# Second biases of the experts by one transpose and one wide matmul in both mixtures of layer 0, and the shared expert four parts later in the first

## The chip, the cores and the metric

The kernel runs on one core of one Trainium2 chip, all in float32. The core has a matrix engine (TensorE; PE in the profile, with its weight loads as PEld), a vector engine (VectorE, DVE), a scalar engine (ScalarE, ACT), a general engine (GpSimd, POOL) and a queue engine (SyncE, SP). Each works through its own list of instructions in order; they wait for each other by semaphores. TensorE writes only to PSUM, a small memory from which DVE and ACT read; GpSimd does not reach it. The metric is the device time of one execution in microseconds (us); lower is better.

## What is computed

The input x is 4 blocks of 512 tokens with 128 channels. It passes through four layers, each a half-weighted mixture or feed-forward part, an attention, and the mixture again. The change touches the two mixtures of layer 0, which share their weights. For one mixture, cut to what matters:

```python
x = x + 0.5 * ffn(layernorm(x))

def ffn(x):                                   # all tokens, 8 experts, 2 of them for each token
    scores = softmax(x @ gate_w.T)
    _, idx = top_k(scores + gate_b, 2)
    comb = (take(scores, idx) one-hot over the experts)     # [token, expert]
    for each expert e:
        h = swiglu((x @ w1[e] + b1[e]) * (x @ w3[e] + b3[e]))
        routed += comb[:, e, None] * (h @ w2[e] + b2[e])
    shared = swiglu((x @ sw1 + sb1) * (x @ sw3 + sb3)) @ sw2 + sb2
    return routed + shared
```

The sum over the experts of comb[:, e] * b2[e], with the shared expert's sb2 as a ninth row, does not need the experts' hidden values. It is one small product for each block: the combination weights (512 tokens by 9) times the second biases (9 by 128).

## The kernel before

One block of 512 tokens is four groups of 128 tokens (NT = 4, P = 128), with the token on the partition. The weights of layer 0 are loaded once. The kernel is written as Python generators: each `yield` ends a part, and the order in which parts are stepped is the order in which instructions are handed to a scheduler. The scheduler puts them in order on each engine by its own estimates, and may move them; only inside the attentions is TensorE's order kept as written (`manual_schedule`). Tiles come from pools with a fixed number of buffers; a new use of a buffer waits for the readers of the old one.

**`route(b)`** (L467) does the routing of one block: layernorm, transpose (L310) and its copy to SBUF (L477), the gate's logits (L485), softmax on ACT and DVE, the rank of each expert for each token (`ranks`, L333 to L338, on DVE), the taken experts (L496), matmuls that count how many tokens stand ahead for each expert (L503, L505), row numbers (L508 to L513), and then eight scatters of 128 rows each by GpSimd into `sorted_x`, sorted by expert (L551). Four closures hold the work on the combination weights:

- `weigh` (L516) sets the ninth column of `comb` to 0.5 on DVE (L517) and the other eight to half the score where the expert is taken (L518), and keeps each token's two shares (L520 to L523).
- `across` (L529) turns `comb`, one group of 128 tokens at a time, with four matmuls against the identity into one PSUM tile of 9 x 512 (L532), and copies it to SBUF on ACT (L533).
- `biases` (L535) multiplies it by the bias rows, again one matmul per group, into a PSUM tile of 128 x 512 (L538).
- `into` (L541) adds that to x on DVE (L321).

`comb` comes from the pool `tiny` with four buffers. In the first mixture the closures run after the eight scatters; in the second, the routes of blocks 0 to 2 are `slow`: they run beside the attention of a later block, and the closures are spread between the scatters.

**`common(b)`** (L563) is the shared expert for one block: eight matmuls of 512 columns (L571) in four pairs, each pair into one two-bank PSUM tile `big` (three buffers), a scaled copy on ACT (L573), products and clamps on DVE (L576 to L584), a sigmoid on ACT (L581), eight matmuls back (L589), and an addition into x (L591). **`fold`** (L594) rewrites the first weights of the eight experts (sixteen matmuls L600, eight copies L601), so that biases ride along, and then loads a row of biases (L603). **`plan`** (L605) computes which expert tile holds what, sends the table through TensorE (L661) to SP and TensorE (L663), and fills the ends of the experts' rooms with zeros (L616). **`tiles`** (L695) then goes through 39 tiles of 128 sorted rows, two at a time: rows fetched by SP (L705), turned (L716), first weights (L726), activation (ACT L729, L738; DVE L733 to L742), turned again (L751), second weights (L759), stored (L763). `places` (L665) computes, on DVE, from which rows each token gathers its results; `back` (L796) gathers them on GpSimd (L807) and adds them (L802).

In the first mixture, the four routes are stepped together, each block four rounds behind the one before, and the chain of `fold` and the four shared experts joins in from round 5:

```python
rest = chain(fold, *shared)
for k in range(24):
    for b in range(B):
        if k >= 4 * b:
            step(routes[b])
    if k > 4:
        step(rest)
```

Between the mixtures stands the attention of layer 0: a head pair at a time, scores (L1035), exponentials on ACT (L1036), sums of them on DVE (L1044), and values (L1049), with the projections of the next pair (L985, L996).

Of the kernel before, what the change touches and what calls it, by code (L numbers as in the profile page):

```python
# [11 lines left out]
F32 = mybir.dt.float32  # L12
# [5 lines left out]
P = 128  # L18
B, S, D = 4, 512, 128
NT = S // P  # L20
EPS = 1e-5
NE = 8
# [104 lines left out]
def laid_out(i):  # L127
    a = {"x": i["L0_attn_x"].reshape(B * S, D)}

    def both(k):  # L130
        return np.concatenate([i[f"L0_ffn_{k}"], i[f"L0_ffn_s{k}"][None]])

    n = NE + 1

    w13 = [both(k).reshape(n, D, L0_I, 2).transpose(1, 0, 3, 2) for k in ("w1", "w3")]
    a["w13"] = np.stack(w13, axis=2)
    b13 = [i[f"L0_ffn_{k}"].reshape(NE, L0_I, 2).transpose(0, 2, 1) for k in ("b1", "b3")]
    a["b13"] = np.stack(b13, axis=1).reshape(1, NE, 2, 2, L0_I)
    for k in ("b1", "b3"):
        a[k] = both(k).reshape(n, 2, P, 2).transpose(2, 0, 3, 1)  # L140
    a["bs"] = np.stack([a[k][:, NE] for k in ("b1", "b3")], axis=1)
    a["w2"] = both("w2").reshape(n, 2, P, D).transpose(2, 0, 1, 3)
    a["b2"] = both("b2")
    a["gate_w"] = i["L0_ffn_gate_w"].T
    a["gate_b"] = i["L0_ffn_gate_b"][None]

    a["w_down"] = np.concatenate([i["L0_attn_w_down_q"], i["L0_attn_w_down_kv"]]).T
    up = []
    for k in ("q", "k"):
        w = i[f"L0_attn_w_up_{k}"]  # L150
        swapped = w.reshape(-1, 2, w.shape[1])[:, ::-1].reshape(w.shape)
        up.append(np.stack([w.T, swapped.T], axis=1))
    a["w_up_qk"] = np.concatenate(up)
    a["w_up_v"] = i["L0_attn_w_up_v"].T
    a["w_up_v_pairs"] = i["L0_attn_w_up_v"].reshape(L0_H // 2, P, 64).transpose(1, 0, 2)
    a["w_out"] = i["L0_attn_w_out"].T.reshape(L0_H // 2, P, D).transpose(1, 0, 2)
    a["ln_scale"] = i["L0_attn_ln_scale"][:, None]
    a["ln_bias"] = i["L0_attn_ln_bias"][:, None]

    a["l1_wqkv"] = np.concatenate([i[f"L1_attn_W{k}"] for k in "qkv"]).T  # L160
    a["l1_bqkv"] = np.concatenate([i[f"L1_attn_b{k}"] for k in "qkv"])[None]
    a["l1_wo"] = i["L1_attn_Wo"].T
    a["l1_bo"] = i["L1_attn_bo"][None]
    a["l1_beta"] = i["L1_attn_beta"][None]
    a["router_w"] = i["L1_ffn_router_w"].T
    a["lora_down"] = i["L1_ffn_lora_down"].reshape(P, D).T
    a["lora_up"] = i["L1_ffn_lora_up"].transpose(0, 2, 1).reshape(P, D)


    def pad_cols(w):  # L170
        out = np.zeros((D, H, 32), np.float32)
        out[:, :, :DH] = w.reshape(D, H, DH)
        return out.reshape(D, NG * P)

    def pad_rows(w):
        out = np.zeros((NJ, 32, NG, D), np.float32)
        out[:, :DH] = w.reshape(NG, NJ, DH, D).transpose(1, 2, 0, 3)
        return out.reshape(P, NG, D)

    def pad_bias(v, one):  # L180
        out = np.zeros((NJ, 32, NG), np.float32)
        out[:, :DH] = v.reshape(NG, NJ, DH).transpose(1, 2, 0)
        out[:, DH] = one
        return out.reshape(P, NG)

    for n, pre, t in (("l2", "L2_attn_W_", False), ("l3", "L3_attn_W", True)):
        w = {k: i[pre + k].T if t else i[pre + k] for k in "qkvo"}
        v = {k: i[pre.replace("W", "b") + k] for k in "qkvo"}
        a[n + "_wq"], a[n + "_wk"] = pad_cols(w["q"]), pad_cols(w["k"])
        a[n + "_bq"], a[n + "_bk"] = pad_bias(v["q"], 0.0), pad_bias(v["k"], 1.0)  # L190

        for k in "qk":
            a[n + "_w" + k + "s"] = w[k].reshape(D, NG, NJ, DH).transpose(0, 2, 1, 3).reshape(D, P)
            a[n + "_b" + k + "s"] = v[k].reshape(NG, NJ, DH).transpose(1, 0, 2).reshape(P, 1)
        a[n + "_wv"], a[n + "_bv"] = w["v"], v["v"][None]
        a[n + "_wo"], a[n + "_bo"] = pad_rows(w["o"]), v["o"][None]
    a["l2_wg"] = i["L2_ffn_Wg"]
    a["l2_w1"] = i["L2_ffn_W1"].transpose(1, 0, 2)
    a["l2_w2"] = i["L2_ffn_W2"].reshape(NE, HID // P, P, D).transpose(2, 0, 1, 3)
    for k in "rkv":  # L200
        a["l3f_w" + k] = i["L3_ffn_W_" + k].T
    a["l3_mu"] = np.stack([i["L3_ffn_mu_r"], i["L3_ffn_mu_k"]], axis=1)
    a.update({"c_" + k: v for k, v in shape_constants().items()})
    return {k: np.ascontiguousarray(v) for k, v in a.items()}
# [34 lines left out]
def program(ctx: ExitStack, tc: tile.TileContext, a: dict, out: bass.AP, worst):  # L239

    nc = tc.nc
# [3 lines left out]
    tiny = SimpleNamespace(tile=lambda *args, **kw: smalls[-1].tile(*args, **kw))  # L245
# [187 lines left out]
    def by_expert(w, rooms, key):  # L433
# [33 lines left out]
        def route(b, work, rows_pool=None, slow=False):  # L467
# [43 lines left out]
            nc.vector.tensor_tensor(mine, m12[:, b], at.unsqueeze(1).to_broadcast([P, 2, NT, NE]), ALU.mult)  # L511
            nc.vector.tensor_reduce(rows[:, b], mine, AX.X, ALU.add)
            nc.vector.tensor_copy(irows[:, b], rows[:, b])  # L513
            comb = tiny.tile([P, NT, NE + 1], F32, tag="comb", name="comb")

            def weigh():  # L516
                nc.vector.memset(comb[:, :, NE], 0.5)  # L517
# [5 lines left out]
                nc.vector.tensor_scalar(share[:, b], share[:, b], 0.5, None, ALU.mult)  # L523


            combT = work.tile([NE + 1, S], F32, tag="combT", name="combT")
            held = []

            def across():  # L529
                pc = one()  # L530
                for t in range(NT):
                    nc.tensor.matmul(pc[: NE + 1, t * P : (t + 1) * P], lhsT=comb[:, t, :], rhs=ident, start=True, stop=True)  # L532
                nc.scalar.copy(combT, pc[: NE + 1, :])  # L533

            def biases():  # L535
                pb = one()
                for t in range(NT):
                    nc.tensor.matmul(pb[:, t * P : (t + 1) * P], lhsT=combT[:, t * P : (t + 1) * P], rhs=w["b2"], start=True, stop=True)  # L538
                held.append(pb)

            def into():  # L541
# [1371 lines left out]
    with tc.tile_pool(name="w0", bufs=1, reuse_waits="tile") as wp:  # L1913
# [9 lines left out]
        else:  # L1923
# [5 lines left out]

            w0["w_up_qk"] = head.tile([P, L0_H * L0_DH], F32, tag="w_up_qk", name="w_up_qk")  # L1930
            behind.append((w0["w_up_qk"], a["w_up_qk"][:, 0, :]))
            w0.update(loads(wp, ["w13", "bs", "w2", "b2"], later=later))
            later += behind
            dram = ctx.enter_context(tc.tile_pool(name="rooms", bufs=1, space=bass.MemoryType.DRAM))
            rooms = [dram.tile([r, D], F32, tag=t, name=t) for t, r in (("sorted_x", ROOM * NE), ("sorted_y", NTL * P))]
# [1 line left out]
            with tc.tile_pool(name="work", bufs=1, reuse_waits="tile") as work:  # L1937
                w0.update(loads(work, ["c_less"]))
                t, src = later.pop(0)
                for e in ((NE, NE + 1), (0, NE // 2), (NE // 2, NE)):  # L1940
                    nc.sync.dma_start(out=t[:, e[0] : e[1]], in_=src[:, e[0] : e[1]])
                w0.update(loads(work, ["c_place", "c_stride"]))
                pairs = load(work, "w_up_v_pairs", later=later)
                for t, src in later[:3]:
                    nc.sync.dma_start(out=t, in_=src)
                mix = by_expert(w0, rooms, 1)
                routes = [mix.route(b, wp, work if b == B - 1 else None) for b in range(B)]
                shared = [mix.common(b, work) for b in range(B)]
                fold = mix.fold()

                rest = chain(fold, *shared)
                for k in range(24):
                    for b in range(B):
                        if k >= 4 * b:
                            step(routes[b])
                    if k > 4:
                        step(rest)
                finish(chain(*routes))
                iwho, places = mix.plan(work)
                finish(rest)  # L1960

                made = {}
                pair01 = {}, {}

                def projected():
                    raw, qk = pair01
                    for n in range(2):
                        raw[n] = l0_project(n, made[0][0], w0, head)
                        yield
                    qk[0] = l0_turned(w0, *raw[0])  # L1970
                    yield

                first, second = chain(places, mix.back(0, wp), l0_begin(0, w0, head, made, 1), projected()), mix.back(1, wp)
                for _ in mix.tiles(work, iwho, later[3:]):
                    if not mix.ready(0):
                        step(places)
                    elif next(first, first) is first and mix.ready(1):
                        step(second)
                values_to_outputs(w0, pairs)
                finish(chain(first, second))  # L1980

                zeros = work.tile([P, D], F32, tag="zeros", name="zeros")
                nc.gpsimd.memset(zeros, 0.0)
                for px, py in pair_rooms:
                    for e in range(NE):
                        nc.sync.dma_start(out=px[e * P : (e + 1) * P, :], in_=zeros)
                        nc.sync.dma_start(out=py[2 * S + e * P : 2 * S + (e + 1) * P, :], in_=zeros)
# [131 lines left out]
```

## Time and profile before

| | us |
|---|---|
| median of 5 runs | 1463.8 |
| lowest and highest run | 1455.44, 1466.82 |
| the profiled execution | 1462.89 |
| its span, first to last instruction | 1461.0 |
| TensorE busy in the span | 1286.4 (88%) |
| DVE busy | 962.8 (66%) |
| ACT busy | 649.7 (44%) |
| POOL busy | 289.9 (20%) |
| L538, 64 records: busy | 9.2 |
| L532, 64 records: busy | 8.9 |
| L533, 8 copies of 9 x 512: mean of one | 0.574 |
| mean granted clock of TensorE, of full speed | 0.926 |

The profile is of one execution, so all places in time below are its own. Stages, in us from its start: first mixture 0 to about 210 (routing and shared expert up to 91, then expert tiles), attention about 210 to 570, second mixture's last block, shared expert and plan about 570 to 623, then its expert tiles. A line of a timeline gives start, length, engine, source line, operation, output and input tiles, shapes, count, and in brackets how long the engine had been idle and what released it. A float32 matmul leaves two records on PE, a transpose one. In the table of stretches, after the stretch and its length come the busy times of PE, PEld, DVE, ACT and POOL with the number of instructions, then the granted clock (1.00 is full speed), the share of the DMA engines and GB/s.

### The profile page before, as it was taken

The numbers are of one execution on the slowest core, as the hardware profiler recorded it, in microseconds if no ns is written. First come the engines' busy times: TensorE is split into PE (matmuls) and PEld (weight loads), VectorE is DVE, ScalarE is ACT, GpSimd is POOL, SyncE is SP. The second block draws the span as 40 slices with busy tenths as digits, with TensorE's granted clock in tenths as the row PEclk, the third lists the DMA queues.
The fourth block names the chain that finished last, engine by engine and source line by source line (L and its number), as shares of the span: only waits on it lengthen the run. The fifth ranks groups of instructions, "written<-read, shape, count | busy, mean of one in ns | idle before, by whom it ended". The sixth has DMA issues, their size and how long they took to land.

```text
span 1461.0 us, 20212 instructions
## 1 busy us (share of the span) xinstructions
PE 1286.4 (88%) x7078; PEld 680.1 (47%) x7078; DVE 962.8 (66%) x2348; ACT 649.7 (44%) x925; POOL 289.9 (20%) x271
## 2 busy tenths in 40 slices
PE   6999889999999999899876598789887899899995
PEld 3556453344353435455544485453554344443233
DVE  4796678989888885876775546467555744355324
ACT  2445436635455453254543242435343436444561
POOL 3510420323112020202343112220212120210000
PEclk9999989999999998999987697899799989989997
DMA  7123211201111020112114000010001000100000
GB/s 271 41 72 98 65 52 58 80 36 71 51 44 72 31 76 1 40 55 60 30 47 168 1 1 1 30 30 1 7 24 29 1 8 22 30 0 9 8 8 11
DMA packets 59970, 63.52 MB, mean 43 GB/s; under 512 B 11082, under 2 KB 51284, under 8 KB 59220
## 3 DMA queue, kind: packets, MB, share of 16 engines
q1 hardware_dynamic: 54228, 50.60, 10.2%
q0 software_dynamic: 5632, 11.55, 2.6%
q8 instruction: 59, 0.97, 0.3%
q14 instruction: 51, 0.41, 0.1%
HBM read 28.69 MB, written 16.65 MB: 31 GB/s over the span
## 4 chain that ended last, share of the span: by engine, by line
PE 67%; DVE 16%; issue 7%; ACT 4%; POOL 3%; DMA 1%; another core or an unknown queue 0%; POOLq 0%; ACTq 0%; DVEq 0%; SPq 0%
PE big L1035 8%; PE one L1049 7%; PE big L1454 7%; PE big L726 6%; PE one L1467 6%; PE big L571 2%; PE one L1078 2%; ACT pT L1457 2%; PE big L985 2%; PE one L759 2%; PE one L1489 2%; PE one L310 2%; PE big L1813 1%; POOL rs L290 1%; PE one L1827 1%
## 5 line engine op out<-in xcount | busy, mean ns | idle before, releaser
L1457 ACT ACTIVATE pT<-big 128x1024 f32<-128x1024 f32 (+3 forms) x256 | 205.7, 865 | 241.8 <-PE big L1454 215.0
L1454 PE MATMUL big<-qkq,qkk 32*128 32x512 f32 (+3 forms) x1024 | 179.3, 583 | 31.3 <-ACT pT L1457 15.7
L1036 ACT ACTIVATE pT<-big 128x1024 f32<-128x1024 f32 x128 | 125.7, 1034 | 55.1 <-PE big L1035 50.2
L726 PE MATMUL big<-w_w,xsT 128*128 x312 | 148.9, 600 | 0.4 <-issue 0.3
L290 POOL TENSOR_TENSOR rs<-rs,root 128x4 f32<-128x4 f32 x51 | 56.9, 1116 | 424.8 <-DVE rs L289 411.1
L1035 PE MATMUL big<-qk 64*128 64x512 f32 x512 | 129.7, 614 | 6.8 <-DVE U L1071 6.8
L1467 PE MATMUL one<-pT,V 128*32 128x512 f32 (+3 forms) x1024 | 126.7, 581 | 1.3 <-DVE pT L1461 0.9
L1454 PEld LDWEIGHTS big<-qkq,qkk 32*128 32x128 f32 x1024 | 65.5, 195 | 120.3 <-ACT pT L1457 45.1
L807 POOL DMA_INDIRECT yg<-sorted_y,ito x64 | 72.2, 1127 | 228.7 <-DMA sorted_y<-ys 152.3
L1049 PE MATMUL one<-pT,V 128*64 128x512 f32 x512 | 116.9, 598 | 0.0
L551 POOL DMA_INDIRECT sorted_x<-xn,irows x64 | 72.5, 1133 | 70.3 <-DVE share L523 23.9
L1044 DVE TENSOR_TENSOR sums<-sums,pT 128x1024 f32<-128x1024 f32 x64 | 78.1, 1221 | 4.8 <-ACT pT L1036 0.4
L1035 PEld LDWEIGHTS big<-qk 64*128 64x128 f32 x512 | 47.3, 189 | 70.2 <-issue 42.3
L1461 DVE TENSOR_TENSOR pT<-pT,w_c_tri 128x256 f32<-128x256 f32 x128 | 51.8, 421 | 36.6 <-ACT pT L1457 31.6
L726 PEld LDWEIGHTS big<-w_w,xsT 128*128 128x128 f32 x312 | 53.9, 193 | 40.0 <-issue 40.0
L1605 DVE COPY U<-one 128x512 f32<-128x512 f32 x32 | 22.1, 689 | 72.5 <-PE one L1467 67.3
L1049 PEld LDWEIGHTS one<-pT,V 128*64 128x64 f32 x512 | 33.9, 136 | 75.2 <-issue 71.2
L1467 PEld LDWEIGHTS one<-pT,V 128*32 128x32 f32 x1024 | 30.0, 118 | 81.4 <-issue 61.1
L733 DVE TENSOR_TENSOR us<-big,t1s 128x1024 f32<-128x1024 f32 (+1 forms) x40 | 47.8, 1194 | 23.8 <-PE one L716 18.8
L571 PE MATMUL big<-xnT,w_w 128*128 128x512 f32 x128 | 60.6, 608 | 3.0 <-DVE u L576 3.0
L1126 ACT COPY U<-one 128x512 f32<-128x512 f32 x32 | 18.8, 587 | 95.0 <-PE one L1049 85.4
L321 DVE TENSOR_TENSOR x<-x,one 128x512 f32<-128x512 f32 x31 | 21.2, 685 | 55.0 <-PE one L1078 19.0
(344 smaller groups left out, 2333.6 us busy)
## 6 DMA issues: line engine op xcount, KB each, us to landing
other<-qk SPq DMA_DIRECT2D x64, 256.0 KB
xs<-sorted_x SPq DMA_DIRECT2D x78, 64.0 KB
sorted_y<-ys SPq DMA_DIRECT2D x38, 128.0 KB
w_w<-in_w SPq DMA_DIRECT2D x2, 2048.0 KB
w_l_w<-in_l_w SPq DMA_DIRECT2D x2, 2048.0 KB
X<-pair_x SPq DMA_DIRECT2D x3, 512.0 KB
pair_y<-y SPq DMA_DIRECT2D x6, 256.0 KB
w_w<-in_w SPq DMA_DIRECT2D x1, 1152.0 KB
```

The source lines that it names most:

```text
L290: nc.gpsimd.tensor_tensor(rs, rs, root, ALU.pow)
L551: apart(nc.gpsimd.indirect_dma_start(out=sorted_x[:, :], out_offset=bass.IndirectOffsetOnAxis(ap=irows[:, b, j, t : t + 1], axis=0), in_=x ...
L571: nc.tensor.matmul(pa[:, m, :], lhsT=w["w13"][:, NE, m, odd, c * P : (c + 1) * P], rhs=xTs[b], start=True, stop=True)
L726: nc.tensor.matmul(pa[:, k, :], lhsT=st[u]["xT"][:, k * P : (k + 1) * P], rhs=w["w13"][:, bass.ds(st[u]["e"][k], 1), m].rearrange("p o a b ...
L807: nc.gpsimd.indirect_dma_start(out=y, out_offset=None, in_=sorted_y[: done(b) * P, :], in_offset=bass.IndirectOffsetOnAxis(ap=ito[:, b, j, ...
L1035: nc.tensor.matmul(sT[:, u, :], lhsT=k[r, t * P : (t + 1) * P], rhs=q[r, :], start=True, stop=True)
L1036: nc.scalar.activation(pT[:, :, t % 2, :], sT, AF.Exp, scale=scale)
L1044: nc.vector.tensor_tensor(s, s, pT[:, :, m, :], ALU.add)
L1049: nc.tensor.matmul(po[r, :], lhsT=V[:, t, :], rhs=pT[:, u, t % 2, :], start=(t == 0), stop=(t == NT - 1), tile_position=(0, 64 * u))
L1454: nc.tensor.matmul(sT[j // 2][:, j % 2, :n], lhsT=kT[r, t * P : (t + 1) * P], rhs=qT[r, S - n :], start=True, stop=True)
L1457: nc.scalar.activation(pT[j2][:, :, :n], sT[j2][:, :, :n], AF.Exp, scale=scale)
L1467: nc.tensor.matmul(po[32 * j : 32 * j + 32, S - n :], lhsT=V[k % 2][:, t, NJ * g + j, :], rhs=pT[j // 2][:, j % 2, :n], start=(t == 0), st ...
```

## The change

The combination weights of a block are laid out with 32 columns for each group of 128 tokens instead of 9, four groups side by side: 128 x 128, of which the unused columns are zero. `across` then needs one transpose, and the turned tile has partition 32 t + e for group t and expert e. The bias rows are laid out by the host as a matrix of 128 x 512 (`b2_wide`), in which row 32 t + e holds expert e's bias in the 128 columns of group t and zeros elsewhere. `biases` is then one matmul of 512 columns with all 128 rows summed. The zeros of `comb` are set by a memset on GpSimd; `comb` gets two buffers instead of four. The load of `b2` becomes one of `b2_wide`. In the first mixture, `fold` and the shared experts join the routes from round 9 instead of round 5.

```diff
@@ laid_out
     a["b2"] = both("b2")
+
+    wide = np.zeros((NT, 32, NT, D), np.float32)
+    for t in range(NT):
+        wide[t, :n, t] = a["b2"]
+    a["b2_wide"] = wide.reshape(P, NT * D)
@@ route
-            comb = tiny.tile([P, NT, NE + 1], F32, tag="comb", name="comb")
+            comb = tiny.tile([P, NT, 32], F32, tag="comb", name="comb", bufs=2)
+            nc.gpsimd.memset(comb, 0.0)
...
-            combT = work.tile([NE + 1, S], F32, tag="combT", name="combT")
+            combT = work.tile([P, P], F32, tag="combT", name="combT")
             held = []
 
             def across():
                 pc = one()
-                for t in range(NT):
-                    nc.tensor.matmul(pc[: NE + 1, t * P : (t + 1) * P], lhsT=comb[:, t, :], rhs=ident, start=True, stop=True)
-                nc.scalar.copy(combT, pc[: NE + 1, :])
+                nc.tensor.transpose(pc[:, :P], comb.rearrange("p t e -> p (t e)"), ident)
+                nc.scalar.copy(combT, pc[:, :P])
 
             def biases():
                 pb = one()
-                for t in range(NT):
-                    nc.tensor.matmul(pb[:, t * P : (t + 1) * P], lhsT=combT[:, t * P : (t + 1) * P], rhs=w["b2"], start=True, stop=True)
+                nc.tensor.matmul(pb, lhsT=combT, rhs=w["b2_wide"], start=True, stop=True)
                 held.append(pb)
@@ program
-            w0.update(loads(wp, ["w13", "bs", "w2", "b2"], later=later))
+            w0.update(loads(wp, ["w13", "bs", "w2", "b2_wide"], later=later))
...
-                    if k > 4:
+                    if k > 8:
                         step(rest)
```

## The prediction

> **What bounds the kernel.** I read the page's share of the chain first, then the chain of waits piece by piece through the two mixtures of layer 0, then the timelines of POOL and DVE where the edit adds a wait, and last the granted clock.
>
> ```profile
> PE 67%; DVE 16%; issue 7%; ACT 4%; POOL 3%; DMA 1%; another core or an unknown queue 0%; POOLq 0%; ACTq 0%; DVEq 0%; SPq 0%
> ```
>
> TensorE carries two thirds of the chain that ends last, so TensorE time taken out is worth something where that chain runs through it, and nothing where DVE ends last. The chain through the first mixture (start us, length us, what) gives the prices:
>
> ```profile
> 39.78 0.97 PE one L532 x8
> ...
> 42.60 1.08 PE one L538 x8
> ...
> 44.74 4.29 PE big L571 x10
> ...
> 50.05 0.49 PE one L310 x4
> ...
> 70.51 8.78 PE big L571 x20
> ```
>
> A matmul leaves two records, a transpose (L310) one. So a block's combination weights cost 0.97 us to turn (L532, four matmuls) and its biases 1.08 us (L538, four). A transpose of 128x128 costs 0.49 / 4 = 0.12 us, and a matmul of 512 columns 8.78 / 10 = 0.88 us.
>
> **What goes.** In a warm stretch a block saves 0.97 - 0.12 = 0.85 us at L532 and 1.08 - 0.88 = 0.20 us at L538: 1.05 us. Block 0 of the first mixture turns half its weights at the start, where TensorE is slow (0.95 us for four records, 0.54 us for the other four; there a transpose costs 0.95 / 4 = 0.24 us): 1.25 + 0.20 = 1.45 us. First mixture: 1.45 + 3 x 1.05 = 4.6 us. Second mixture: three blocks inside the attention, 3.15 us, and the last block 1.05 us. In all 8.8 us of TensorE.
>
> The trace has no transpose of this tile in this place. Its dearest neighbour is the 0.24 us of the slow stretch, its cheapest 0.11 us (a single L310 record at 38.48); I take 0.12 us, since seven of eight stand in warm stretches. *The Trainium skill's "TensorE: Matmul & The Clock Gate", Part 4, gives a transpose about 275 ns inside a kernel. By that the eight would cost 1.2 us more; the chain here shows four in 0.49 us, and the row decides.*
>
> **What comes, at no cost.** The copy of the turned weights on ACT shrinks from 512 columns (0.57 us) to 128; a copy of 256 columns takes 0.37 us (L719), so at least 0.2 us goes, off the path. The bias weights grow from 4.5 KB to 256 KB at the same place of SP's queue. The DMA engines move 370 to 420 GB/s there, so everything behind (weights of the attention, first used after 155 us) comes 0.6 us later; L538 first needs them at 35 us, and the traffic ends at 31. The second load moved on SP, w_up_v_pairs, now stands behind the fold's bias row (45.8 us) and is used at 211 us. The listing of the changed kernel's instructions shows that the scheduler undoes most of the "four parts later": all sixteen fold matmuls still precede the first shared-expert matmul, but all eight of block 0's now run before block 2's counting (L503), where five did.
>
> **What comes, with a wait.** The eight memsets of the weights' tile run on POOL (a 128x128 memset takes 0.20 us) and the tile has two buffers instead of four. DVE's small memset of the shared column (L517) now waits for POOL's. By the listing, block 2's and block 3's POOL memsets stand behind the eight scatters of blocks 0 and 1, and DVE's L517 stands in the middle of the ranking of blocks 1 and 2, between L334 and L335.
>
> ```profile
> 40.67 0.97 POOL L551 DMA_INDIRECT sorted_x<-xn,irows  x1 [0.72 <-POOL xn L480]
> ...
> 49.86 0.97 POOL L551 DMA_INDIRECT sorted_x<-xn,irows  x1 [0.30 <-issue]
> ...
> 81.24 0.20 POOL L1983 MEMSET zeros<- 128x128 f32 x1 [2.57 <-DMA sorted_x<-zeros]
> ```
>
> Eight scatters of a block hold POOL for 10.2 us (40.67 to 50.83). Block 0's end at 31.2: DVE waits until about 31.5 in block 1's ranking, needs 1.9 us more, and TensorE wants the result only at 34.9. Hidden; without those 1.5 us of cover each further us would count. Block 1's is the one that matters.
>
> ```profile
> 45.73 0.42 DVE L334 TENSOR_TENSOR eq<-biased 128x256 f32<-128x256 f32 x1
> ...
> 46.32 0.42 DVE L335 TENSOR_TENSOR eq<-eq,w_c_lower 128x256 f32<-128x256 f32 x1
> ```
>
> TensorE's savings on blocks 0 and 1 (2.5 us) bring its first shared-expert matmul from 44.74 to 42.3, and L334 to an end at 44.8. The scatters start 0.6 us earlier, at 40.1, end at 50.3, and the memset is done at 50.8. DVE stands still for 6.0 us. Behind L517 stands the first L576, which empties a PSUM buffer of the shared expert. There are three: TensorE fills them by 42.3 + 3 x 1.75 = 47.5 and waits until 51.5; then it waits for the ranking again (53.3 to 54.4). So L335 comes 4.6 us later than before.
>
> How much is won back? Before, DVE takes from L335 at 46.3 to the first expert tile's L733 at 96.6, 50.3 us, of which it is idle 5.3 (2.4 at 52.1, 0.6, 0.6, 0.9 and three small ones): 45.0 us of work, and 0.5 us of it moves behind L733. From 50.9 that ends at 95.4 if DVE never idles. Followed by hand through the new order it idles 1.8 us: 97.2, 0.6 us late, while TensorE, having less to do, starts its tiles 0 to 1.7 us early. So the 4.6 us of the first mixture are eaten. From the tiles on TensorE is busy without a gap (one pair of tiles in 5.0 us), and the difference is passed on.
>
> Then there is the clock. In the table by stretches (busy us of PE, PEld, DVE, ACT, POOL; then granted clock, DMA):
>
> ```profile
> 164.00:168.00 4.00, 0.34 (x1) 0.00 (x0) 3.62 (x11) 1.53 (x2) 2.44 (x3) 1.00 0.00 0
> 168.00:172.00 4.00, 1.83 (x5) 1.15 (x6) 3.78 (x9) 0.46 (x1) 3.09 (x4) 0.58 0.16 45
> 172.00:176.00 4.00, 4.00 (x16) 2.90 (x16) 1.72 (x3) 1.03 (x3) 1.65 (x2) 0.56 0.13 39
> ```
>
> An idle stretch of four us was followed by some seven us at about half clock. My stall is as long. Such a stretch costs between nothing (DVE is behind anyway) and 3.5 us. *"TensorE: Matmul & The Clock Gate", "Why this matters for your kernels", warns of gaps over about 3 us; by its window of 3.4 us the loss would be 1.7 us, and it speaks against this change.* For the first mixture as a whole I take +0.5 us, between -1.7 and +4.
>
> Inside the attention TensorE is the bound: the chain runs from piece to piece on it, and both old steps stand in it.
>
> ```profile
> 364.11 0.97 PE one L532 x8
> ...
> 369.58 1.08 PE one L538 x8
> ```
>
> Of the 3.15 us I take 2.8: block 3's L517 waits there for POOL until its scatters end (454.1 before), some 1.5 us in a stretch in which DVE has 1 us in 5 to spare. Bounds: 0 (DVE is 90% busy) and 3.15. In the second mixture's last part DVE ends last (TensorE waits 1.6 us for L576, 1.1 for L584, 1.7 for the first tile's rows); of 1.05 us I take 0.5, between -1.5 and +1.5, because the listing puts the tile table's matmuls (L661) behind four shared-expert matmuls.
>
> **Sum.** +0.5 - 2.8 - 0.5 = -2.8 us. The profiled execution took 1462.9 us (span 1461.0), so 1460.1 for it; the median of five runs is 0.9 us higher: **1461 us**.
>
> **Rivals.**
> - *The whole gain arrives* (17%). POOL comes to the memset in time, or DVE catches up: -4.6 - 3.15 - 1.05 = -8.8, 1455 us. For it: 5.3 us of idle DVE to catch up in. Against: the order of POOL's queue.
> - *The new wait costs more than the savings* (20%). DVE's 4.6 us late are passed on to the tiles, and the clock drops: +4.6 + 1.7 - 3.15 = +3.2, 1467 us. It decides when the first tile's matmul (L726, 91.05 us before) comes later than about 94.
> - *The attention gives nothing* (13%): DVE sets its pace, so +0.5 - 0.5 = 0, 1464 us. Against: TensorE waits there for DVE only 6 us in 200.
> - My forecast: 50%.
>
> **Range and chances.** Repeated runs of the old kernel lie between 1455 and 1467. The bounds above and that spread give 1452 to 1469 us. What a measurement of this kernel can tell from no change is about 0.5%, 7.3 us: only the full gain passes it on one side (0.17 with the forecast's edge), the second rival's upper bound on the other (0.09); within it 0.74.
>
> **What would show it.** Right: a wait of 5 to 6 us of DVE's L517 on POOL's memset near 45 us, TensorE idle some 4 us near 48, the first L726 between 89 and 92.5, the distance from block 1's attention to block 3's shorter by about 1 us per block. Wrong: L517 without a wait; a first L726 at 87 (full gain) or past 94; a drop of clock after the stall that lasts over 7 us; attention of unchanged length.

## The result, and the profile after

The changed kernel took 1463.25 us (median of 36 runs, 1453.64 to 1469.44), the kernel before, beside it, 1462.68 us (62 runs). The ratio is 1.0006, 95% interval 0.9995 to 1.0017: no difference that this kernel's measurement can tell. The forecast said 1461 and "within 0.5%", and that came true. The 2.8 us of gain in that 1461 did not come: the interval ends at -0.7 us. Several steps of the forecast failed, and they are the lesson. The profiled execution took 1462.11 us (span 1460.3).

The share of the chain that ends last, from the page after:

```profile
PE 61%; DVE 20%; issue 8%; ACT 4%; POOL 3%; DMA 1%; another core or an unknown queue 0%; POOLq 0%; SPq 0%; DVEq 0%; ACTq 0%
```

TensorE was busy for 1276.5 us, 9.9 less than before. Its share of the chain went from 67% to 61%, DVE's from 16% to 20%: in this execution the chain passes more through DVE. The line numbers after are larger by about five: L517 is now L523 (memset of the shared column), L532 is L537 (transpose), L538 is L542 (wide matmul), L571 is L575, L576 is L580, L335 is L340, L726 is L730.

First the wait. POOL's timeline in the first mixture after, the end of block 1's scatters and the memset for block 3, and under it DVE's timeline there:

```profile
47.00 0.97 POOL L555 DMA_INDIRECT sorted_x<-xn,irows  x1 [0.30 <-issue]
48.28 0.97 POOL L555 DMA_INDIRECT sorted_x<-xn,irows  x1 [0.30 <-issue]
49.23 0.25 POOL L520 MEMSET comb<- 128x128 f32 x1
```

```profile
42.88 0.42 DVE L339 TENSOR_TENSOR eq<-biased 128x256 f32<-128x256 f32 x1
49.54 0.06 DVE L523 MEMSET comb<- 128x4 f32 x1 [6.24 <-POOL comb L520]
49.60 0.75 DVE L580 SCALAR_TENSOR_TENSOR u<-big,w_bs,t 128x512 f32<-128x512 f32 x1
50.27 0.42 DVE L340 TENSOR_TENSOR eq<-eq,w_c_lower 128x256 f32<-128x256 f32 x1
```

A memset of 0.06 us stops DVE for 6.24 us, in the middle of block 2's ranking and ahead of the L580 that would empty a PSUM buffer of the shared expert. TensorE's timeline, and the table by stretches (busy us of PE, PEld, DVE, ACT, POOL, then granted clock):

```profile
40.36 5.31 PE L575 MATMUL big<-xnT,w_w 128*128 128x512 f32 x12
50.41 3.78 PE L575 MATMUL big<-xnT,w_w 128*128 128x512 f32 x4 [4.74 <-DVE u L580]
...
54.27 1.85 PE L510 MATMUL one<-taken,w_c_ones 128*128 128x32 f32 x8
```

```profile
44.00:48.00 4.00, 1.67 (x4) 0.38 (x2) 0.00 (x0) 1.96 (x2) 3.06 (x4) 1.00 0.14 49
48.00:52.00 4.00, 1.59 (x2) 0.84 (x3) 2.46 (x7) 0.94 (x2) 1.19 (x2) 0.70 0.10 33
52.00:56.00 4.00, 4.00 (x14) 2.69 (x12) 2.30 (x9) 0.95 (x2) 0.00 (x0) 0.50 0.00 0
56.00:60.00 4.00, 4.00 (x15) 2.86 (x15) 2.04 (x8) 0.85 (x2) 1.07 (x2) 0.50 0.00 0
60.00:64.00 4.00, 4.00 (x8) 2.00 (x8) 1.39 (x7) 1.54 (x2) 3.09 (x3) 0.59 0.15 51
```

TensorE reaches the shared expert at 40.36 us instead of 44.57, fills its buffers by 45.67 and stands for 4.74 us. Then it goes at half clock until about 63 us: L510's eight records take 1.85 us where they took 1.04 before, two matmuls of L575 take 3.78 instead of about 1.8. The first tile's matmul comes at 97.17 us instead of 91.05.

In the attention there is a second wait of the same kind, which the forecast had placed elsewhere. DVE's timeline at block 1's attention, TensorE's at that block's end:

```profile
368.78 0.61 DVE L806 SCALAR_TENSOR_TENSOR x<-yg,share,x 128x128 f32<-128x128 f32 x2
373.97 0.06 DVE L523 MEMSET comb<- 128x4 f32 x1 [4.58 <-issue]
```

```profile
391.68 1.14 PE L1073 MATMUL big<-rsum,w_c_spread 32*128 32x512 f32 x8 [1.51 <-DVE rsum L1065]
```

DVE waits 4.58 us for POOL's memset of block 2's weights, which stands behind block 0's eight scatters and three gathers and ends at 373.9. (The line names "issue" and not POOL; DVE starts 0.07 us after POOL's end, and in the second profile the same wait, again 4.58 us, is put down to POOL.) DVE enters the end of the block late, and TensorE waits there 1.51 us for the reciprocal sums (0.71 before).

By stage the two profiles differ, after against before, by +6.1 us at the first tile, +6.2 at the end of the attention, -0.2 at the second mixture's first tile, -0.7 at the end of the span. How much of that is the change a second pair of profiles must say.

### The profile page after: what moved, and what is told of

Its sections match the earlier page's. It is cut to its first block, busy times and chain, and to the rows that moved or that the text cites. A ratio compares the mean times of both kernels' runs of the same rounds, so it can differ in the third digit from the quotient of the medians.

```text
span 1460.3 us, 20011 instructions
## 1 busy us (share of the span) xinstructions
PE 1276.5 (87%) x6974; PEld 671.7 (46%) x6974; DVE 960.8 (66%) x2348; ACT 647.2 (44%) x925; POOL 292.6 (20%) x279
## 4 chain that ended last, share of the span: by engine, by line
PE 61%; DVE 20%; issue 8%; ACT 4%; POOL 3%; DMA 1%; another core or an unknown queue 0%; POOLq 0%; SPq 0%; DVEq 0%; ACTq 0%
PE big L1458 7%; PE big L730 6%; PE big L1039 6%; PE one L1053 6%; PE one L1471 6%; PE one L1082 2%; ACT pT L1461 2%; PE big L989 2%; PE big L575 2%; PE one L763 2%; PE one L1493 2%; PE one L315 1%; PE big L1817 1%; POOL rs L295 1%; PE one L1831 1%
## 5 line engine op out<-in xcount | busy, mean ns | idle before, releaser
L730 PE MATMUL big<-w_w,xsT 128*128 x312 | 152.2, 611 | 0.4 <-issue 0.3
L1471 PE MATMUL one<-pT,V 128*32 128x512 f32 (+3 forms) x1024 | 122.6, 566 | 1.3 <-DVE pT L1465 0.9
L730 PEld LDWEIGHTS big<-w_w,xsT 128*128 128x128 f32 x312 | 54.3, 194 | 40.9 <-issue 40.7
L575 PE MATMUL big<-xnT,w_w 128*128 128x512 f32 x128 | 62.9, 629 | 6.2 <-DVE u L580 6.2
```

The lines of the kernel that those rows point to most:

```text
L575: nc.tensor.matmul(pa[:, m, :], lhsT=w["w13"][:, NE, m, odd, c * P : (c + 1) * P], rhs=xTs[b], start=True, stop=True)
L730: nc.tensor.matmul(pa[:, k, :], lhsT=st[u]["xT"][:, k * P : (k + 1) * P], rhs=w["w13"][:, bass.ds(st[u]["e"][k], 1), m].rearrange("p o a b ...
L1471: nc.tensor.matmul(po[32 * j : 32 * j + 32, S - n :], lhsT=V[k % 2][:, t, NJ * g + j, :], rhs=pT[j // 2][:, j % 2, :n], start=(t == 0), st ...
```

## The experiments

Each number is the time against the kernel before on the same chip. Its median there lay between 1446.9 and 1462.1 us, depending on the chip, so only ratios are compared between groups; "us" is the ratio less one, times that median. The last column is the start of the first tile's matmul (L726 of before) in the run's one profile. Three profiles whose code is that of before up to there have 89.06, 90.89 and 91.05, so differences under 2 us in that column are scatter.

| run | wide | waits for POOL | round | ratio (95%) | us | first tile |
|---|---|---|---|---|---|---|
| b_again (before) | no | none | 5 | 0.9992 (0.9976–1.0009) | -1.2 | 90.89 |
| a_again (changed) | yes | both mixtures | 9 | 1.0028 (1.0011–1.0045) | +4.1 | 96.79 |
| b_wait | no | both mixtures | 5 | 1.0139 (1.0114–1.0163) | +20.1 | 107.88 |
| b_wait1 | no | first mixture | 5 | 1.0064 (1.0043–1.0085) | +9.3 | 95.89 |
| b_k8 | no | none | 9 | 1.0025 (1.0006–1.0045) | +3.7 | 95.09 |
| b_more | 3 x narrow | none | 5 | 1.0090 (1.0067–1.0113) | +13.0 | 89.06 |
| a_dve | yes | none | 9 | 0.9980 (0.9960–0.9999) | -2.9 | 87.22 |
| a_once | yes | second mixture | 9 | 1.0054 (1.0033–1.0074) | +7.8 | 95.87 |
| a_once_dve | yes | none | 9 | 0.9963 (0.9944–0.9982) | -5.4 | 88.15 |
| a_wait1 | yes | first mixture | 9 | 0.9988 (0.9971–1.0006) | -1.8 | 97.55 |
| a_once_dve_k4 | yes | none | 5 | 0.9948 (0.9926–0.9969) | -7.6 | 87.07 |
| a_k4 | yes | both mixtures | 5 | 1.0011 (0.9991–1.0030) | +1.6 | 100.65 |

**The wait alone**, in the kernel before:

```diff
-            comb = tiny.tile([P, NT, NE + 1], F32, tag="comb", name="comb")
+            comb = tiny.tile([P, NT, NE + 1], F32, tag="comb", name="comb", bufs=2)
+            nc.gpsimd.memset(comb, 0.0)
```

> The kernel before with the new wait alone: POOL's memset of the weights' tile (36 columns) and two buffers instead of four; the matmuls and their order on TensorE are those of before. Theory (the wait is what eats the first mixture's saving): DVE's memset of the shared column for block 3 waits for POOL until block 1's eight scatters end, about 50.8 us, so L340's counterpart in block 2 comes 4 to 5 us later than 46.3, and the first tile's matmul (91.05 us before) comes at 95 to 97; total 3 to 6 us above before (ratio 1.002 to 1.004). Rival A (DVE wins it back from its 5.3 idle us): the wait is there, but the first tile comes at 91 to 92, ratio 1.000. Rival B (what followed the wait in the profiled execution was a drop of the clock that is chance): first tile later only if the clock falls below 0.7 within 50 to 60 us.

Measured: +20 us, far over the theory's 3 to 6. DVE stops three times: to 51.35 us as expected, and twice more. DVE's timeline of this run:

```profile
66.53 0.18 DVE L363 TENSOR_REDUCE sm<-ex 128x4 f32<-128x32 f32 x1 [4.30 <-ACT t L574]
66.55 0.06 DVE L518 MEMSET comb<- 128x4 f32 x1
86.77 0.06 DVE L518 MEMSET comb<- 128x4 f32 x1 [6.07 <-POOL comb L515]
```

These are the second mixture's first two tiles of weights. Nothing in them depends on the first mixture, so the scheduler had hoisted their memsets, on POOL behind the scatters of blocks 2 (to 66.3 us) and 3 (to 86.5). The first line names ACT, whose work had ended at 65.86 us; the memset that starts beside it shows that POOL, done at 66.48, was the one. In the changed kernel POOL's two memsets are hoisted as well (69.31 and 84.71 us), but DVE's two stand at 106.53 and 107.38, so nothing waits for them. The edit also halves the buffers; that alone is not the stop, since the run with the memset on DVE (below) has two buffers as well and none.

With the memset in the first mixture only (`if key == 1:` before it):

> The kernel before with the new wait alone, and in the first mixture alone: POOL's memset of the weights' tile and two buffers in the first mixture; in the second no memset. TensorE's order is that of before. The same edit in both mixtures cost 18.6 us and showed three stalls of DVE behind POOL: to 51.4 us (first mixture's block 3, behind block 1's scatters), to 66.5 and to 86.8 us (the second mixture's first two tiles of weights, whose memsets the scheduler had put behind the scatters of blocks 2 and 3). Theory: only the first stall is left, first tile's matmul 4 to 7 us later than in before, total 4 to 7 us over before (ratio 1.003 to 1.005). Rival (the first stall alone brings all that follows, by the clock): first tile over 12 us later, total 12 to 18 us over before.

Measured: +9.3 us (interval 6.2 to 12.3, six runs) with the first stall alone, first tile 5.0 us later. The total came out over the theory's 7 us and under the rival's 12. So a stop of 4.3 us is not won back: it costs 5.0 us by the first tile. What comes on top is not settled: against the second profile of before, its profile is 6.8 us late at the second mixture's first tile, 1.6 of it by a drop of the clock at 392 us, where nothing waits for POOL, and only 3.7 us at the end.

**TensorE time in the attention**, priced by adding it:

```diff
-                for t in range(NT):
+                for t in [*range(NT)] * (3 if slow else 1):
```

in both `across` and `biases`.

> The kernel before, with the old turning of the weights and the old product with the biases each written three times instead of once in the three blocks that run inside the attention (the repeats write the same values): 16 extra matmuls for each of three blocks, 2 x (0.97 + 1.08) = 4.1 us each, 12.3 us in all. It prices TensorE time in just the two places from which the change takes it. Theory (TensorE sets the pace there, as predicted): total 9 to 12.3 us above before, ratio 1.006 to 1.0085, each block's attention 3 to 4.1 us longer. Rival (the attention gives nothing, DVE sets its pace): ratio 1.000 to 1.002. In between: the part that is passed on, times the 3.15 us that the change saves there, is what the attention gave.

Measured: +13.0 us (interval 9.7 to 16.4) for 12.3 us of priced matmuls. Each of the three blocks is longer by 3.5 us where the matmuls stand, 10.6 in all; in this profile two drops of the clock (0.57 at 480 to 484 and at 548 to 552 us) add 1.7 us each. The rival is out: the attention passes TensorE time on.

**The wide matmul without the wait.** First the memset on DVE (`nc.vector.memset(comb, 0.0)`):

> The changed kernel with one word changed: the memset of the weights' tile on DVE instead of POOL, so that nothing of DVE waits behind the scatters. Theory (the wait ate the first mixture's saving): no idle DVE of over 2 us between 44 and 50 us, first tile's matmul at 87 to 91 us instead of 97.2 in the changed kernel and 91.05 before, total 4 to 8 us below before (ratio 0.9945 to 0.9975). The eight memsets cost DVE about 0.2 us each. Rival (DVE is the bound of the first mixture anyway): first tile at 91 to 93 us, total 2 to 4 us below before. Rival (the attention takes no gain on): 0 to 3 us below before.

Measured: -2.9 us, first tile at 87.22 us. That is 10 us earlier than in the changed kernel, and DVE is idle for over 2 us nowhere between 40 and 60. So the wait and the first tile are as the theory has them; the total is not: it is short of the 4 to 8 us and inside the rivals' ranges (interval 0.1 to 5.8 us below before). Then the zeros written once:

```diff
+        combs = [kept([P, NT, 32], f"comb{i}") for i in range(2)]
+        for comb in combs:
+            nc.gpsimd.memset(comb, 0.0)
...
-            comb = tiny.tile([P, NT, 32], F32, tag="comb", name="comb", bufs=2)
-            nc.gpsimd.memset(comb, 0.0)
+            comb = combs[b % 2]
```

> The changed kernel with the zeros written once: two tiles of weights kept through a mixture, zeroed by POOL at its start, and a block uses the tile of the block two before; its nine columns are overwritten, so the zeros stay. No memset stands behind scatters; the order on TensorE shifts a little. Theory: as with the memset on DVE, no wait near 45 us, first tile's matmul at 87 to 91 us, total 4 to 8 us below before (ratio 0.9945 to 0.9975). Rival: DVE bounds the stage, first tile at 91 to 93, total 2 to 4 us below before.

Measured: +7.8 us, a miss. The edit took the wait out of the first mixture and left the second mixture's two memsets on POOL, hoisted behind scatters. DVE's timeline of this run shows it, again under the name of something else ("issue") and beside POOL's memset at 61.32:

```profile
61.59 0.42 DVE L585 TENSOR_SCALAR u<-u 128x512 f32<-128x512 f32 x1 [6.82 <-issue]
61.62 0.06 DVE L525 MEMSET comb<- 128x4 f32 x1
```

With the same zeros written by DVE (`nc.vector.memset` in those lines):

> The changed kernel with the zeros written once for each mixture, by DVE instead of POOL, into two tiles that the blocks use in turn: four memsets of about 0.17 us in all, and nothing of DVE behind POOL. Theory (the run with POOL's zeros written once was slow because the second mixture's two memsets stood behind the scatters of blocks 2 and 3, and DVE waited to 61.6 us for them): no such wait, first tile's matmul 1 to 3 us earlier than in before, total 2 to 6 us below before (ratio 0.996 to 0.9985), as with the memset on DVE. Rival (the two kept tiles or the order of TensorE cost it): first tile later than in before, total 3 to 8 us above.

Measured: -5.4 us, first tile at 88.15. One word moves the time by 13 us, and the miss is explained: it was the wait for POOL, not the kept tiles.

**Two profiles of one chip.**

> The kernel before once more, unchanged: a second profile, on the same chip as the other three runs of this group. It tells which of the differences between the two first profiles are the change and which are differences between executions. Theory: the stretch from the end of layer 0's attention to the second mixture's first tile (560 to 623 us in the first profile) is 4 to 5 us shorter here too, with nothing changed, since two kernels whose code there is that of before were shorter by 4.5 us; the cold spell at 209 to 217 us is absent. Rival: both stretches are as in the first profile; then the saving there belongs to the change.

Measured: the stretch from the attention's end to the second mixture's tiles is 5.1 us shorter in this second profile of the unchanged kernel, and the cold spell from 209 us on (5.2 us) is gone. So the -6.4 us that the first pair showed in the second mixture's last part was mostly not the change.

> The changed kernel once more, unchanged, on the same chip as the second profile of before. Theory: the stall of DVE for POOL near 44 to 50 us and the drop of the clock after it are there again, first tile's matmul 6 to 8 us later than in the second profile of before; each of the three blocks of the attention that hold the change is 0.7 to 0.8 us shorter; total within 0.3% of before. Rival: the clock's drop was chance, the first tile is 2 to 5 us later only, and the total is 2 to 5 us under before.

Measured: +4.1 us. The theory's 0.3% includes it only just (the interval goes to 0.45%), the stall is there (6.24 us again), the clock falls to 0.50 for eight us, and the first tile is 5.9 us late, just short of the theory's 6 to 8. Against the second profile of before the stages are +5.9 us (first tile), +6.2 (start of block 1's attention), +6.3 (end of the last attention), +5.3 (second mixture's first tile), +6.1 (end of the span).

**Wait in the first mixture only**, TensorE's order that of the changed kernel:

```diff
-            nc.gpsimd.memset(comb, 0.0)
+            (nc.gpsimd if key == 1 else nc.vector).memset(comb, 0.0)
```

> The changed kernel with POOL's memset in the first mixture and DVE's in the second; TensorE's order is that of the changed kernel from end to end. Theory: two waits cost the changed kernel its gain, the one near 44 to 50 us and one of 4.58 us in the attention (DVE's memset of block 2's shared column behind POOL's, behind block 0's scatters), which made TensorE wait 0.8 us longer at that block's end and was followed by a clock drop of 1.56 us. So here the first tile's matmul is 5 to 7 us later than in before, as in the changed kernel, but the attention's three blocks give 2.2 us net and no step of over 1 us back at block 1's end, total 0 to 3 us above before, some 2 us under the changed kernel. Rival: the clock drop at the end of block 1's attention is chance and not the wait's (it was seen in the kernel before with the first mixture's wait alone, too): then the step of 1.56 us is here as well.

Measured: -1.8 us, below the theory's 0 to 3. The first tile is as late as in the changed kernel, but the three attention blocks give 0.74 us each, and the step of 2.4 us back at 391 us is absent. That step holds 0.8 us for the late reciprocal sums, which are the wait's, and some 1.6 us for a drop of the clock, which is not shown to be the wait's: b_wait1, with no wait there, shows it at the same place, and a_k4 (308 us) and b_more (480 us) show it at the end of other blocks where nothing waits for POOL.

**The move of four parts**, alone and taken out:

> The kernel before with the fold and the shared experts joining from round 9 instead of round 5, and nothing else. Theory: no difference beyond 2 us either way (ratio 0.9985 to 1.0015), first tile's matmul within 1 us of 91 us. Rival A: the move alone gains 2 us or more in the first mixture, so that part of what the run without waits won is the move's. Rival B: it loses 2 us or more, so that the wide matmul won more than was seen.

Measured: +3.7 us, the first tile 4 us later: rival B. TensorE's and DVE's timelines of this run:

```profile
23.88 12.82 PE L600 MATMUL big<-w_w,w_c_less 128*128 128x512 f32 x26
36.63 1.15 PE L538 MATMUL one<-w_b,combT 9*128 9x128 f32 x8
```

```profile
37.82 0.69 DVE L321 TENSOR_TENSOR x<-x,one 128x512 f32<-128x512 f32 x1 [9.44 <-PE one L538]
```

Before, the first four fold matmuls ran at 20.82 us, ahead of the second half of block 0's turning. Now thirteen stand in one row behind all of it, and block 0's biases end 1.5 us later; DVE's idle time from 20 us up to there is nearly the same in sum (12.7 us, 9.44 of it in one piece, against 11.9 before, 6.82 and 3.84 of it). The rest of the 4 us comes in the shared experts, in another order there: DVE waits 2.11 us for TensorE at 75.80, TensorE 2.13 us at 79.17. Which of these is the cause was not tried.

> The changed kernel with the zeros written once for each mixture by DVE, and with the fold and the shared experts joining from round 5 as in before: the wide matmul without the move of four parts. Theory: the move did little (the scheduler undid most of it), so the time is within 2 us of the run with round 9, which was 6.5 us under before: ratio 0.9945 to 0.998. Rival: the move was part of the gain (block 0's eight small matmuls ahead of block 2's counting): first tile's matmul 2 us or more later than with round 9, ratio 0.998 to 1.000.

Measured: -7.6 us (interval -10.8 to -4.5), the fastest version: faster than before and than the changed kernel. Taking the move out is worth 2.2 us here (the two runs are on different chips), in one direction with b_k8 but inside the two intervals.

> The changed kernel with the fold and the shared experts joining from round 5, as in before: the wide matmul and its waits for POOL, without the move. Theory (three terms that add up: the wide matmul gains about 8.7 us, as in the run without waits and without the move; the waits cost 8 to 10 us; the move costs 3.6 us, as in the run of the move alone): total within 2 us of before, ratio 0.9985 to 1.0015, about 3 us below the changed kernel; DVE waits for POOL near 50 us and again by 4 to 5 us in the attention. Rival (the terms do not add up: without the move the scatters start at another time and the wait is longer or shorter): ratio over 1.003 or under 0.997, with the wait near 50 us over 8 us or under 3 us.

Measured: +1.6 us, and the totals do add up: the wide matmul -7.6 (a_once_dve_k4) and the waits +9.5 (a_again less a_once_dve, both from round 9) give +1.9. That is 2.5 us under the second measurement of the changed kernel and 0.7 over the first. The stages fit less well, so part of the agreement is luck: the wait near 50 us is 3.32 us, the one in the attention 4.59, but there is a third, 5.21 us up to 66.59, behind the second mixture's first hoisted memset (POOL's at 66.31), and the first tile is the latest of all with the wide matmul. Built from single edits, the whole change is -7.6 (wide), +9.3 (b_wait1) and +3.7 (b_k8): +5.4, against +4.1 in the second and +0.9 in the first measurement of the changed kernel. This takes b_wait1 and not b_wait (+20.1), since the two later stops of b_wait are absent from the changed kernel; every term has an interval of some 3 us either way.

## Why the prediction was right, and where it was wrong

**The total was right, its path was not.** Two large terms cancel, the saving on TensorE and the wait for POOL, and the forecast knew both. It gave the saving as -8.8 at most, and the run without waits and without the move gives -7.6 (4.5 to 10.8). It put the wait at 5.1 us in the first mixture (4.6 saved, +0.5 left) and 0.35 in the attention; the waits cost 9.5 us against a_once_dve, 7.0 against a_dve. By stage, in the second pair of profiles, the first mixture is +5.9 for the forecast's +0.5, the attention about 0 for -2.8, the last part -1 for -0.5. Three of the forecast's own signs of being wrong came true: a first tile past 94, a drop of the clock over 7 us, an attention of unchanged length. That the total still fell inside 0.5% is luck as far as the path goes: 0.5% is 7.3 us, wider than these errors came to in the time.

**The size of the savings.** The terms were 0.85 (turning) and 0.20 (biases) a block, 1.05 in all. In the attention it is 0.74 in every run with the change. TensorE's timeline in the second profile of before, and in the run with zeros written once by DVE:

```profile
358.44 1.04 PE L532 MATMUL one<-w_c_ident,comb 128*9 128x128 f32 x8
359.41 2.85 PE L1035 MATMUL big<-qk 64*128 64x512 f32 x12
...
363.90 1.15 PE L538 MATMUL one<-w_b,combT 9*128 9x128 f32 x8
364.99 3.65 PE L1049 MATMUL one<-pT,V 128*64 128x512 f32 x16
```

```profile
354.86 0.33 PE L539 MATMUL one<-w_c_ident,comb 128*128 128x128 f32 x1
355.12 2.85 PE L1041 MATMUL big<-qk 64*128 64x512 f32 x12
...
359.61 1.12 PE L544 MATMUL one<-w_b_wide,combT 128*128 128x512 f32 x2
360.66 3.65 PE L1055 MATMUL one<-pT,V 128*64 128x512 f32 x16
```

From start to next start, the turning went from 0.97 to 0.26 us, the biases from 1.09 to 1.05. In the mixtures the same two instructions, each alone as well, cost what the forecast took. From the changed kernel's first mixture, block 3:

```profile
71.53 0.31 PE L537 MATMUL one<-w_c_ident,comb 128*128 128x128 f32 x1
71.67 1.02 PE L575 MATMUL big<-xnT,w_w 128*128 128x512 f32 x2
72.53 1.02 PE L542 MATMUL one<-w_b_wide,combT 128*128 128x512 f32 x2
73.39 1.95 PE L593 MATMUL one<-w_w,h 128*128 128x128 f32 x16
```

Here it is 0.14 and 0.86 us, and 0.11 and 0.85 in the second mixture's last block (595.60 us), for the forecast's 0.12 and 0.88. So the price depends on the neighbours and not on standing alone, and the mis-sized term is the attention's: its -3.15 should have been 3 x 0.74 = -2.2 without its wait. What in the attention makes both dearer was not tried. The last part's -0.5 was about -1 (539 to 612 us in the second pair). *The Trainium skill's "TensorE: Matmul & The Clock Gate", Part 4, gives about 275 ns for a transpose (of bf16) inside a kernel. The forecast weighed that and let the row of four decide; from start to next start a transpose of float32 has 0.26 us here in the attention, near the page, and 0.11 to 0.14 us in the mixtures at full clock, near the row.*

**The wait of the first mixture** was where the forecast put it: 6.24 us for 6.0, TensorE idle for 4.74 us. The wait behind block 0's scatters, which the forecast called hidden, is hidden: DVE stops for 6.34 us up to 32.01, and TensorE does not pause. The step that failed is the next one, that DVE wins the delay back: "if DVE never idles", with 1.8 us idle by hand for 5.3 before. DVE's first waits in the changed kernel after the stall:

```profile
56.16 0.19 DVE L513 TENSOR_TENSOR at<-one,allb 128x32 f32<-128x32 f32 x1 [1.86 <-PE one L510]
60.53 0.19 DVE L359 TENSOR_REDUCE mx<-one 128x4 f32<-128x32 f32 x1 [2.33 <-PE one L490]
63.80 0.69 DVE L326 TENSOR_TENSOR x<-x,one 128x512 f32<-128x512 f32 x1 [2.08 <-PE one L542]
```

In this profile DVE is idle for another 9.3 us between the stall and the first tile, always waiting for TensorE: the 6.3 us of these three lines while TensorE runs at half clock, and 3.0 later, at full clock (0.61, 0.16, 1.04, 1.17 us). In the second profile it is 5.2 us, for 3.7 in the second profile of before. So the idle time grew in both pairs where the forecast let it shrink to a third. The forecast had the clock's drop as 0 to 3.5 us that DVE, being behind, would cover. But the ranking goes back and forth between the two engines, so a slow TensorE makes DVE idle. The drop is not the whole of it: in b_wait1 the two stretches of four us after the stop have a clock of 0.77 and 0.80, not 0.50, and the first tile is still 5.0 us late. How the delay divides between the stop and the clock stays open. The first mixture came to +5.9 us, over the forecast's bound of +4, and the second rival's own condition (a first tile later than 94) was met: 97.17 and 96.79. *"TensorE: Matmul & The Clock Gate", "Why this matters for your kernels", warns of gaps over about 3 us; the trace agrees, with a gap of 4.74. The estimate of 1.7 us from its window was too little: TensorE ran at half clock for some 13 us in the first profile and 9 in the second.*

**The wait of the attention** was forecast as 1.5 us for block 3's weights. That wait is there (2.41 us in the first profile, 1.13 in the second) and costs TensorE nothing in the second pair. The one that costs is of 4.58 us, for block 2's, since POOL has gathers in its queue too. Its cost is between 0.8 and 2.4 us.

**The move** was put among the edits "at no cost". Alone it costs 3.7 us (0.9 to 6.6); beside the wide matmul the difference is 2.2 us and inside the intervals. The new order of the fold matmuls against block 0's biases was read in the listing, and not priced. (In the same paragraph, w_up_v_pairs is used from 202.2 us on, L976, and not from 211; nothing hangs on it.)

**The rivals.** "The attention gives nothing" came true in the sum of the changed kernel (+6.2 and +6.3 at its ends), but by a second wait and a drop of the clock, not because DVE sets the pace. "The whole gain arrives" is what the kernel without waits and without the move does: -7.6 against the -8.8 written for it.

**What stays open:** whether the clock's drop at 392 us follows from the wait (the same drop comes without one in b_wait1, a_k4 and b_more), and why the kernel is 1% faster on some chips (some 10 us of it, between the two profiles of before, in two stretches that the change does not touch).

## What to carry to other kernels

Zeros that never change should be written by the engine that writes the rest of the buffer, not by a memset that joins the queue of an engine with long transfers; whether they are written once or each time (-5.4 and -2.9 us here) the intervals do not part. A scheduler may hoist such a memset, and the small instruction that waits for it, into another stage, so look for its every occurrence in the other engines' order. Price an instruction among the neighbours that it will have, from start to next start: one transpose cost 0.11 us in one stage and 0.26 in another. And do not count idle time of before as time to catch up in: here the engine that was late went on waiting for the one that it had held up.

## What the runs showed of the hardware

- POOL takes an indirect scatter each 1.28 us in the first mixture, so what stands behind eight of them waits 10 us. In the attention eight took 12.4 us, and three gathers behind them 3.7 more (357.6 to 373.7).
- After a stop of 4.74 us TensorE ran at half clock for some 13 us (9 in the second profile), though the profile shows it busy for nearly all of that time (4.00 of 4.00 us at clock 0.50, twice).
- The clock also falls for four us (to 0.57) where TensorE only pauses for 0.7 to 1.1 us three times (b_wait1 at 392 us, a_k4 at 308, b_more at 480), and once where it does not pause (b_more at 548). The second profile of before has the same instructions as b_wait1 there and no drop. Each is worth 1.6 to 1.7 us.
- A transpose of 128x128 in float32 costs 0.10 to 0.15 us from start to next start between the mixtures' matmuls at full clock and 0.26 between the attention's; a matmul of 512 columns 0.85 to 0.95 and 1.05.
- One kernel's median was 1446.9 us on some chips and 1462.1 on others, more than the change is worth.
